# A scheduled graph-layer kernel: own PSUM tiles for the first group, held end products, rows two ahead, sums and normalising at other times, and idle turns of the identity

## The chip, the cores and the metric

The kernel runs on one core of one Trainium2 chip. The metric is the device time of one execution in microseconds (us). Several executions of each kernel were timed. "Same" is a difference of less than 2%.

## The reference

A graph layer on x of shape (32, 512, 256) with a 0/1 matrix adj of (32, 512, 512), all in float32:

```python
h = jnp.maximum(_layernorm(x, axis=-1), 0.0)
xc = jnp.transpose(h, (0, 2, 1))
c = relu(_bn(_conv1d(xc, conv1_w, 0), ...))          # 256 -> 256, 1 tap
c = _bn(_conv1d(c, conv2_w, 8), ...)                 # 256 -> 256, 17 taps
x_conv = jnp.transpose(relu(c + xc), (0, 2, 1))
s = h @ w_se.T + b_se                                # 3 columns
dist = sq[:, :, None] + sq[:, None, :] - 2.0 * einsum('bnd,bmd->bnm', s, s)
A = jnp.exp(-dist) * adj
msg = relu(h @ w_msg.T + b_msg)
x_nmp = einsum('bnm,bmd->bnd', A, msg)
x_in = concatenate([x_conv, x_nmp], -1)
gi, gh = x_in @ w_ih.T + b_ih, h @ w_hh.T + b_hh     # 3 gates of 256 each
r, z = sigmoid(gi_r + gh_r), sigmoid(gi_z + gh_z)
n = tanh(gi_n + r * gh_n)
return x + (1 - z) * n + z * h
```

## The kernel before

The 17-tap convolution is done in seven groups of 25 products with transformed inputs and weights. Around the products stand four other kinds of work for TensorE: **begins** (a batch is normalised and turned into hT), **rows** (conv1 for the batches of a group), **graphs** (messages, exponentials, and the sum over neighbours, xnb) and **gates**. A small scheduler, run while the program is built, decides the order in which all of this is written down: it keeps a clock `now` of TensorE's planned time, and each stream tells it either a time or a condition before which it must not go on. On the chip every engine then works through its own list in that fixed order. A plan that is wrong about a time therefore becomes a wait.

The first group's products share one tile of two PSUM banks. Later groups make a middle product (copied to `mid` by ScalarE) and then two "end" products:

```python
if g == 0:
    two = cps.tile([P, 2, N], F32, name="ps_c")
...
    if g == 0:
        ps, mid = two[:, n % 2, :nz], None
        product(ps[:, :nh], (0, *d0), (1, *d1))
        hand()                      # sums of the product before
        yield now
        product(ps[:, nh:], (0, *d1), (1, *d2))
    else:
        psb = bps.tile([P, N], F32, name="ps_b")[:, :nh]
        product(psb, (2, x2[:, 1, :], 0))
        mid = cv.tile([P, NH], F32, name="mid", bufs=2)[:, :nh]
        act.activation(mid, psb, AF.Copy)
        hand()
        yield now
        ps = cps.tile([P, 2, N], F32, name="ps_c")[:, :, :nh]
        for k in range(2):
            product(ps[:, k, :], (k, XD[m][:, k, :], 0))
```

hT goes through DRAM: GpSimd issues the store when a batch is begun, SyncE issues the load when the rows of its group are due. When a batch is normalised is decided by `norm_ahead`:

```python
def begin(b):
    ...                                          # b >= TURNED
    for o in range(ND):
        dve.transpose(HT[b][:, o, :], xb[:, o, :])
    nc.gpsimd.dma_start(HD[b], HT[b])            # store hd<-hT
    begun = b + 1

def all_rows():
    ...
    for g in range(1, NG):
        for b in batches(g):
            yield lambda: freed >= g - 1 and begun > b
            rows_wait = True
            load_row(b)                          # load hT<-hd on SyncE's queue
            yield now + 8.0
            yield from rows(g, b)
            rows_wait = False

def norm_ahead(early=0.45):
    for b in list(NORMS)[:2]:
        if (b < G or clock["conv"] >= (b - G) / PER - early) and norm_some(b):
            return True
    return False

streams = {
    "rows": (all_rows(), 1e9, -2.0),
    "begins": (all_begins(), 1.05 * PER, -0.15),
    "graphs": (all_graphs(), 11.5 * PER, 0.0),
    "conv": (convolution(), 80.0, 0.0),
    "gates": (all_gates(), 31.25 * PER, 1.6),
}
```

The stream that may go on and has the smallest clock goes next; the last number is where its clock starts.

## Time and profile before

| | before |
|---|---|
| time, 3 runs when the prediction was made | 2156.06 us median, 2148.67 to 2158.63 |
| span of the profiled run | 2155.2 us |
| matmul work, every record at its undisturbed spacing | 2007 us |
| loss (span less that work) | 148 us |

How to read it: TensorE is the bound, and the prediction below shows its lines of the profile. The busy share (96%) is too kind, because a matmul at half clock counts as busy for twice as long. The number used in this document is therefore the **loss**: the length of a stage less the matmul work done in it, each matmul record at the spacing that it has in the trace when nothing disturbs it. The stages are those of the prediction: to the first product, the groups, and the end.

### The profile page before, as it was taken

How to read it: one execution, taken by the hardware profiler on the slowest of the kernel's cores; microseconds unless marked ns; L12 is line 12 of the kernel's file. 1: busy time of each engine (PE TensorE's matmuls, PEld its weight loads, DVE VectorE, ACT ScalarE, POOL GpSimd, SP SyncE). 2: the span in 40 equal slices, each digit the busy share in tenths (PEclk: the TensorE clock that was granted, in tenths of full speed). 3: DMA queues.
4: the chain of work that ended last, by engine and by line, in shares of the span. 5: the costliest groups of instructions: out<-in, count | busy, mean ns of one | idle time of the engine just before them, and what ended most of it. 6: DMA issues, size and time to landing. Idle time of an engine off the chain costs nothing. (4 is left out here: it accounts for less than half of the span.)

```text
span 2155.2 us, 25648 instructions
## 1 busy us (share of the span) xinstructions
PE 2062.0 (96%) x8632; PEld 1259.6 (58%) x8632; DVE 1512.9 (70%) x2660; ACT 762.4 (35%) x1271; POOL 336.7 (16%) x582
## 2 busy tenths in 40 slices
PE   8888799999998999999999999999999999999998
PEld 4776465665654566665656655665656666654443
DVE  6777478777876667886777776877767777754333
ACT  5534533235322425233344234442242522143111
POOL 2100112112111112110121111111110211111111
PEclk9999899999999999999999999999999999999999
DMA  7335776676767658777577677676745656544331
GB/s 276 142 132 173 256 225 183 197 214 189 245 167 191 185 154 227 208 211 208 145 214 201 178 215 208 184 208 172 214 118 156 192 147 167 161 123 99 93 93 40
DMA packets 546436, 383.07 MB, mean 178 GB/s; under 512 B 456576, under 2 KB 473472, under 8 KB 545664
## 3 DMA queue, kind: packets, MB, share of 16 engines
q1 hardware_dynamic: 512992, 282.17, 49.5%
q0 software_dynamic: 28624, 86.01, 11.5%
q10 hardware_dynamic: 4688, 13.24, 1.6%
q8 instruction: 69, 1.13, 0.2%
q14 instruction: 63, 0.52, 0.1%
HBM read 281.95 MB, written 99.35 MB: 177 GB/s over the span
## 5 line engine op out<-in xcount | busy, mean ns | idle before, releaser
L135 PE MATMUL ps_acc<-xnb,wih 128*128 128x512 f32 (+1 forms) x772 | 364.9, 595 | 6.9 <-DMA xnb<-nd 6.9
L135 PE MATMUL ps_acc<-xconv,wih 128*128 128x512 f32 (+1 forms) x772 | 363.4, 593 | 2.7 <-ACT xconv L126 2.7
L135 PE MATMUL ps_acc<-hTb,whh 128*128 128x512 f32 x768 | 355.9, 593 | 1.0 <-ACT r L126 1.0
L135 PE MATMUL ps_c<-xd,w 128*128 128x135 f32 (+1 forms) x2400 | 308.3, 282 | 19.2 <-DVE n L126 9.0
L135 PEld LDWEIGHTS ps_c<-xd,w 128*128 128x128 f32 x2400 | 294.0, 193 | 22.3 <-issue 14.3
L1012 POOL DMA_DIRECT2D out_dram<-res x252 | 163.8, 657 | 771.8 <-DVE res L126 651.2
L135 PEld LDWEIGHTS ps_acc<-xnb,wih 128*128 128x128 f32 x772 | 143.1, 191 | 163.8 <-issue 149.3
L135 PEld LDWEIGHTS ps_acc<-xconv,wih 128*128 128x128 f32 x772 | 143.7, 190 | 160.7 <-issue 154.9
L135 PEld LDWEIGHTS ps_acc<-hTb,whh 128*128 128x128 f32 x768 | 141.8, 190 | 156.0 <-issue 146.4
L135 PE MATMUL ps_g<-at,msg 128*128 128x512 f32 x512 | 226.6, 592 | 1.8 <-DVE at L126 1.8
L135 PEld LDWEIGHTS ps_b<-x,w 128*128 128x128 f32 x1200 | 160.3, 191 | 67.2 <-issue 54.2
L126 DVE TENSOR_TENSOR r<-ps_acc,r 128x512 f32<-128x512 f32 (+1 forms) x65 | 44.4, 683 | 212.1 <-PE ps_acc L135 212.1
L135 PE MATMUL ps_b<-x,w 128*128 128x135 f32 (+1 forms) x1200 | 164.9, 280 | 7.7 <-ACT at L126 3.6
L135 PEld LDWEIGHTS ps_g<-at,msg 128*128 128x128 f32 x512 | 96.2, 190 | 117.5 <-issue 112.4
L126 ACT ACTIVATE mid<-ps_b 128x270 f32<-128x270 f32 (+1 forms) x150 | 59.7, 398 | 261.9 <-PE ps_b L135 261.7
L126 DVE SCALAR_TENSOR_TENSOR x<-x,x 128x544 f32<-128x544 f32 (+5 forms) x161 | 137.6, 855 | 2.9
L126 DVE TENSOR_TENSOR msg<-ps_g,bmsg 128x256 f32<-128x256 f32 x128 | 53.8, 421 | 113.1 <-PE ps_g L135 112.4
L135 PE MATMUL ps_g<-hT,w 128*128 128x512 f32 (+4 forms) x288 | 124.1, 576 | 4.8 <-DMA hT<-hd 3.7
L126 DVE TENSOR_TENSOR x<-x 128x272 f32<-128x272 f32 (+5 forms) x280 | 127.7, 497 | 0.3
L126 ACT ACTIVATE z<-ps_acc,brz 128x512 f32<-128x512 f32 x64 | 43.9, 687 | 233.3 <-PE ps_acc L135 225.2
L135 PE MATMUL ps_g<-wmsg,hTg 128*128 128x259 f32 x496 | 125.9, 382 | 0.0
L135 PE MATMUL ps_c<-x,w 128*128 128x116 f32 x800 | 105.5, 289 | 20.9 <-ACT z L126 9.9
(112 smaller groups left out, 2582.4 us busy)
## 6 DMA issues: line engine op xcount, KB each, us to landing
w<-wd SPq DMA_DIRECT2D x125, 768.0 KB, 5.7
m_sb<-in_adj_dram SPq DMA_DIRECT2D x384, 64.0 KB, 3.1
hd<-hT POOLq DMA_DIRECT2D x32, 512.0 KB, 5.6
hT<-hd SPq DMA_DIRECT2D x32, 512.0 KB, 5.5
hTb<-hd SPq DMA_DIRECT2D x32, 512.0 KB, 5.1
xnb<-nd SPq DMA_DIRECT2D x64, 256.0 KB, 3.3
xconv<-cd SPq DMA_DIRECT2D x32, 512.0 KB, 5.3
res<-in_x_dram SPq DMA_DIRECT2D x256, 64.0 KB, 3.1
```

Of the source, the lines that this page charges most:

```text
L126: getattr(self.engine, name)(*tiles, **more)
L135: nc.tensor.matmul(ps, lhsT, rhs, **more)
L1012: queue.dma_start(OB[b][:, s.start // 32 : s.stop // 32, o * P + 32 * g : o * P + 32 * g + 32], y[at, s].rearrange("i (k j) -> i k j", j=32),)
```

## The change

Its intent is to close the holes on TensorE in the first third. Its short description names five things: the first group's products in their own tiles, the end products held until their banks are free, rows loaded two ahead, graph sums ahead, and the identity turned while TensorE waits. The diff has more than that: a new rule for when a batch is normalised (`told` is the number of batches whose messages are made), a limit on how many parts stand before their stores, and two moves in the gates.

```diff
-    cps = ctx.enter_context(tc.tile_pool(name="cps", bufs=1, space=PSUM))
+    first_ctx = ExitStack()
+    cps = first_ctx.enter_context(tc.tile_pool(name="cps", bufs=2, space=PSUM))
...
+    def keep_warm(n):
+        for _ in range(n):
+            nc.tensor.transpose(unused[:, :P], ident, ident)
...
     def load_row(b):
-        HR[b] = front.tile([P, ND, N], F32, name="hT", bufs=2)
-        nc.sync.dma_start(HR[b], HD[b])
+        if b not in HR:
+            HR[b] = front.tile([P, ND, N], F32, name="hT", bufs=2)
+            nc.sync.dma_start(HR[b], HD[b])
+            HR_AT[b] = now + 8.0
...
-        if now < t or act.free > now + 0.3:
+        if now < t or act.free > now + 0.3 or len(PARTS) > 2 and now < PARTS[-3]:
             return False
...
+        act.free += 0.7
+        PARTS.append(act.free + 4.0)
...
                 sums.send(got)
+                handed = dve.free + LAG
...
-            if g == 0:
-                two = cps.tile([P, 2, N], F32, name="ps_c")
+            if g == 1:
+                first_ctx.close()
+                cps = ctx.enter_context(tc.tile_pool(name="cps2", bufs=1, space=PSUM))
...
-                    ps, mid = two[:, n % 2, :nz], None
+                    ps, mid = cps.tile([P, N], F32, name="ps_c")[:, :nz], None
...
                     hand()
-                    yield now
+                    yield handed
                     ps = cps.tile([P, 2, N], F32, name="ps_c")[:, :, :nh]
...
-    def norm_ahead(early=0.45):
+    def norm_ahead():
         for b in list(NORMS)[:2]:
-            if (b < G or clock["conv"] >= (b - G) / PER - early) and norm_some(b):
+            if (b < G or told >= b - 3) and norm_some(b):
...
                 rows_wait = True
-                load_row(b)
-                yield now + 8.0
+                for k in (b, b + 1):
+                    if k in batches(g) and k < begun:
+                        load_row(k)
+                yield HR_AT[b]
                 yield from rows(g, b)
-                rows_wait = False
+                del HR[b]
+                rows_wait = b + 1 in HR
...
-        "graphs": (all_graphs(), 11.5 * PER, 0.0),
+        "graphs": (all_graphs(), 11.5 * PER, -0.5),
...
+    keep_warm(16)
...
+            waits += 1
+            if waits > 2 and not HB:
+                keep_warm(2)
```

Left out: a flag `turning` that keeps a row from starting in the middle of a begin; in the first batch's gates a pause of 8 us and the hidden products set ahead of the residual; the same new rule where `norm_ahead(0.25)` was called; and a new planned length of a matmul (`max(0.223, 0.005 + elements / 600)` in place of `max(0.22, elements / 600)`), which shifts every planned time a little.

More of the change, by code (lines that the diff above doesn't have):

```diff
@@ L133, in matmul @@
         nonlocal now
-        now += max(0.22, elements(ps) / 600.0)
+        now += max(0.223, 0.005 + elements(ps) / 600.0)
         nc.tensor.matmul(ps, lhsT, rhs, **more)
@@ L158, in settle @@
             LATER.pop(0)[1]()
-    XS, HT, HB, HR, HG, XN, XR = {}, {}, {}, {}, {}, {}, {}
+    XS, HT, HB, HR, HR_AT, HG, XN, XR = {}, {}, {}, {}, {}, {}, {}, {}
     NORMS, NORM_AT = {}, {}
@@ L639, in summed @@
         yield
-    EVAC = []
+    EVAC, PARTS = [], []
     def batches(g):
@@ L665, in evacuate @@
         if o == ND - 1 and last == U:
-            evacuated[b] = act.free + 4.0
+            evacuated[b] = PARTS[-1]
         return True
@@ L705, in convolution @@
     def convolution():
-        nonlocal at_product
+        nonlocal at_product, cps
         def product(ps, *terms):
@@ L720, in product @@
                 )
-        done = None
+        done, handed = None, 0.0
         def hand():
-            nonlocal done
+            nonlocal done, handed
             if done is not None:
@@ L880, in begin @@
     def begin(b):
-        nonlocal begun
+        nonlocal begun, turning
         if b >= TURNED:
@@ L894, in begin @@
             HT[b] = front.tile([P, ND, N], F32, name="hT", bufs=2)
+            turning = True
             for o in range(ND):
@@ L899, in begin @@
             nc.gpsimd.dma_start(HD[b], HT[b])
-            begun = b + 1
+            begun, turning = b + 1, False
             if b + 2 < B:
@@ L907, in begin @@
         yield NORM_AT[b]
+        turning = True
         for d in range(ND):
@@ L910, in begin @@
             if d == ND - 1:
-                begun = b + 1
+                begun, turning = b + 1, False
                 if b < 2 or b >= G:
@@ L962, in gates @@
         load_sums(b, 1)
+        if b == 0:
+            yield now + 8.0
         hT = HB[b]
@@ L1049, in gates @@
             ps_r = acc.tile([P, N], F32, name="ps_acc")
+            ps_h = None
             if o == 0:
-                if b not in XC:
-                    yield lambda: b in evacuated
-                    yield evacuated[b]
-                    load_conv(b)
-                yield XC_AT[b]
-                residual(b)
-                yield from products(ps_r, o, 0, 0, 1, (0, 2))
+                if b not in RES:
+                    yield from products(ps_r, o, 0, 0, 1, (0, 2))
+                    ps_h = acc.tile([P, N], F32, name="ps_acc")
+                    yield from products(ps_h, o, 2, 0, 1, (0, 0))
+                    if b not in XC:
+                        yield lambda: b in evacuated
+                        yield evacuated[b]
+                        load_conv(b)
+                    yield XC_AT[b]
+                    residual(b)
+                else:
+                    yield from products(ps_r, o, 0, 0, 1, (0, 2))
                 yield lambda: RES[b] < 1e9
@@ L1063, in gates @@
             yield from products(ps_r, o, 0, 1, 3, (0, 2), reset)
-            ps_h = acc.tile([P, N], F32, name="ps_acc")
-            yield from products(ps_h, o, 2, 0, 1, (0, 0), reset_hidden)
+            if ps_h is None:
+                ps_h = acc.tile([P, N], F32, name="ps_acc")
+                yield from products(ps_h, o, 2, 0, 1, (0, 0), reset_hidden)
+            else:
+                reset_hidden()
             ps_z = acc.tile([P, N], F32, name="ps_acc")
@@ L1108, in background @@
         nonlocal turn_of
-        if norm_ahead(0.25):
+        if norm_ahead():
             return True
@@ L1139, in all_begins @@
             yield from begin(b)
-    rows_wait = False
+    rows_wait = turning = False
     def all_rows():
@@ L1150, in all_rows @@
             for b in batches(g):
-                yield lambda: freed >= g - 1 and begun > b
+                yield lambda: freed >= g - 1 and begun > b and not turning
                 if b == batches(g)[0]:
@@ L1154, in all_rows @@
                 rows_wait = True
-                load_row(b)
-                yield now + 8.0
+                for k in (b, b + 1):
+                    if k in batches(g) and k < begun:
+                        load_row(k)
+                yield HR_AT[b]
                 yield from rows(g, b)
-                rows_wait = False
+                del HR[b]
+                rows_wait = b + 1 in HR
     def all_gates():
@@ L1177 @@
     hold = {name: None for name in streams}
+    unused, waits = acc.tile([P, N], F32, name="ps_acc"), 0
+    keep_warm(16)
     load(0)
@@ L1214 @@
         name = min(able, key=lambda k: clock[k])
+        waits = 0
         hold[name], began = None, now
```

## The prediction

> **What bounds the kernel now.** I read the page first (shares, slices), then a table of busy time by stage, then TensorE's waits by stage, then the order of time around single waits.
>
> The page's shares and two rows of its 40 slices (one slice is 54 us):
>
> ```profile
> PE 2062.0 (96%) x8632; PEld 1259.6 (58%) x8632; DVE 1512.9 (70%) x2660; ACT 762.4 (35%) x1271; POOL 336.7 (16%) x582
> ...
> PE   8888799999998999999999999999999999999998
> ...
> PEclk9999899999999999999999999999999999999999
> ```
>
> TensorE is the bound, but not evenly: all slices that are not full lie in the first third. I cut the span at the products' groups (the last of the first group's 25 products ends at 223.6 us, of the second's at 484.7, of the third's at 781.6; from 1899.2 only graph sums and gates are left). Columns: stretch, length, busy time of TensorE, its weight loads, VectorE, ScalarE, GpSimd (instructions), granted clock, DMA share, GB/s.
>
> ```profile
> 0.00:46.50 46.50, 36.69 (x117) 19.53 (x118) 28.80 (x83) 30.48 (x63) 10.47 (x31) 0.96 0.77 282
> 46.50:223.60 177.10, 152.31 (x1020) 128.18 (x1019) 134.45 (x271) 78.03 (x148) 16.36 (x28) 0.95 0.47 159
> 223.60:272.00 48.40, 37.25 (x111) 19.05 (x111) 25.11 (x44) 25.49 (x40) 6.75 (x12) 0.86 0.72 240
> 272.00:484.70 212.70, 200.39 (x996) 136.46 (x995) 167.83 (x310) 66.49 (x119) 40.84 (x72) 0.99 0.71 207
> 484.70:781.60 296.90, 274.93 (x1130) 167.17 (x1129) 213.92 (x368) 103.44 (x178) 46.37 (x76) 0.97 0.68 190
> 781.60:1899.20 1117.60, 1112.73 (x4649) 675.55 (x4649) 836.33 (x1419) 395.24 (x639) 170.91 (x291) 1.00 0.67 185
> 1899.20:2155.20 256.00, 247.69 (x620) 113.70 (x618) 106.45 (x169) 63.25 (x85) 45.00 (x72) 0.99 0.37 91
> ```
>
> Length less busy time gives TensorE's idle time by stage: 9.8, 24.8, 11.2, 12.3, 22.0, 4.9, 8.3; in all 93. The first 781.6 us hold 80 of it; the last 8.3 are the drain after the last matmul. Busy time hides more, because it also counts time in a reduced clock. So I weighed every matmul by its undisturbed distance to the next one in this trace (429 ns for a record of 512 columns, 219 for 259, 115 for 135, 112 for 116, 109 for a transpose; a matmul is two records, a transpose one). That sums to 2007 us. The span is 148 us longer: 19 before the first product, 40 in the first group, 34 in the second (with the passage from 223.6 to 272), 32 in the third, 15 in all the rest, 8 in the drain. **What a change can win lies in the first 782 us, about 125 us.**
>
> Who ends the waits there (line, who was waited for: us, times, longest):
>
> ```profile
> PE ps_c L135 <- ACT z L126: 9.9, 13, 2.5
> PE ps_c L135 <- DVE n L126: 9.0, 3, 4.4
> PE ps_c L135 <- ACT n L126: 7.7, 10, 2.5
> PE ps_g L140 <- ACT x_sb L126: 7.1, 1, 7.1
> PE ps_acc L135 <- DMA xnb<-nd: 6.9, 3, 6.3
> PE ps_b L830 <- ACT right L126: 6.3, 2, 5.0
> PE ps_c L135 <- issue: 5.1, 2, 2.7
> PE ps_g L135 <- DMA hT<-hd: 3.7, 1, 3.7
> ...
> PE ps_c L135 <- DVE z L126: 3.4, 1, 3.4
> ```
>
> The first and third line all fall in the first group. One such wait in the order of time:
>
> ```profile
> 77.95 1.94 PE L135 MATMUL ps_c<-x,w 128*128 128x116 f32 x16
> ...
> 79.92 0.56 ACT L126 ACTIVATE z<-ps_c 128x464 f32<-128x464 f32 x1 [3.75 <-PE ps_c L135]
> ...
> 80.53 2.04 PE L135 MATMUL ps_c<-x,w 128*128 128x116 f32 x16 [0.65 <-ACT z L126]
> ```
>
> The copy of the product before starts only when the first half (16 records) of this product is done, and the second half waits for that copy: 0.56 us plus about 0.1. Both products share one tile of two banks; the recorded dependencies are the tile's, not the bank's.
>
> **What the Trainium skill says.** (1) "PSUM — Partial Sum Buffer", section on bank collisions: two engines must be kept apart by bank and quadrant; different banks run clean. So the 0.65 us wait is not one the chip needs, and two tiles of one bank each remove it. The trace cannot show the rule itself; it shows the wait. (2) "TensorE: Matmul & The Clock Gate", Part 1: after an idle window of about 3.4 us the clock is halved until a busy window has passed. This trace agrees: it granted 0.50 from 147.2 to 157.4 us, after a stretch (144.0 to 147.2) with only 0.93 us of TensorE busy time, and 16 records of 116 columns then took 3.76 us in place of 1.94. (3) Same page, Part 4: transposes do not count as busy for that clock. If so, turning the identity while waiting warms nothing. This trace does not decide it, as no window in it is filled by transposes alone.
>
> **The change part by part.**
> Own tiles: 23 waits, 9.9 + 7.7 = 17.6 us, become none, because a tile is written again only two products later. I count 15 won, as a faster TensorE meets VectorE more often.
> Ends held (the two end products are issued only when the sums have taken the last pair out of its bank): the same waits in the second and third group, "DVE n" 9.0, "issue" 5.1, "DVE z" 3.4, and 1.7 for ps_b, together 19. The hold only lets gates or sums go first; VectorE's backlog behind it (4.4 us at 596 to 600) stays. I count 12.
> Passage 223.6 to 272: the 5.0 us wait for "right" came about because ScalarE, which works in order, stood before it at a part whose buffer was still being stored (waits of 0.16 and 1.35 us for that transfer, 1.3 us for each part). The change issues a part only when its buffer should be free. Then 2.7 for the first residual (now after the hidden products) and 1.2. In the new order the second group's first product follows the first group's last at once, with 4 transposes between, where before 12 matmuls for rows, 12 for sums, 8 for messages and 6 of the gates stood there. I count 9 of 11.2.
> Rows two ahead, graph sums ahead: the waits for hT (3.7) and for xnb (6.3 + 0.4) are transfers started too late; 10.4 us, I count 9.
> Clock: the granted share says what was lost, (1 - 0.95) x 177 = 8.9, 0.14 x 48.4 = 6.8, 0.01 x 213 + 0.03 x 297 = 11, and 1.9 at the start: 28.6. The drops follow waits of 2 us and more, most of them in the list above, so they go with these; I count 15 without any help from the identity, since other idle windows remain.
> Sum of gains: 15 + 12 + 9 + 9 + 15 = 60.
> Costs: 124 identity transposes, 38 before the first hT product and 34 more before the first group; 30 of them stand ahead of the first real transpose. The identity is ready at 1.8 us; at 109 ns each they end by 5.1, at half clock by 8.3 us, against 7.06 for the data: 0 to 1.3 us late. The other 52 stand where the plan sees TensorE idle; 2 us in all for those that sit wrongly. VectorE: I counted, by order of both programs and the measured median durations, what stands before the last product of the first group: TensorE's work there rises from 137 to 169 us, VectorE's from 147 to 158 (sums of durations, some 8% above busy time, as they overlap). In the second group they fall from 227 to 206 and from 213 to 207. So VectorE is nearly as loaded as TensorE in both, and I take off 6 us for new waits on it.
> Net 60 - 8 = 52: **2156 - 52 = 2104 us**. Check by stage: first product at 46 (31 us of work), first group 169 + 17 = 186, second 206 + 22 = 228, third 275 + 16 = 291, the remaining 1325 + 13 of loss, drain 8: 2097. The two agree within what I can claim.
>
> **Rivals.**
> R1, VectorE takes over: with the shared tile gone, products come as fast as their operands and weights do, and waits turn from "ACT n, z" to "DVE x", "ACT w", "DVE n". For: 158 against 169 us in the first group. Against: before, only 3.2 us of waits there were for operands or weights, and VectorE runs at 75% between 781 and 1899 us without stopping TensorE. Then the groups one and two win little: about 2130.
> R2, the idle time only moves: work pulled forward into the first group leaves less to fill the second, whose holds then find nothing to issue. Time about 2125.
> R3, the identity does hold the clock: most of the 28.6 us come back and the start warms earlier; about 2090.
> R4, transfers pulled ahead collide in the first 60 us (DMA share 0.77): a few us lost; 2110.
>
> **Range and chances.** The line for 2% is 2113. The floor is 2007 + 7 for the first data + 8 drain = 2022; losses of 60 to 110 us are plausible after: 2080 to 2132. Most of my weight is on the plain case, a third on R1 or R2. A slowdown would need the late, full stages to suffer, and their order hardly changes. Faster 0.64, same 0.35, slower 0.01.
>
> **What would show it.** Right: no wait of ps_c on ACT n or z near 0.65 us, those two lines under 4 us together; xnb and hT waits gone from 650 to 760; the last first-group product ends near 232 and the third group's near 750; granted clock above 0.98 up to 780. Wrong: a sum of waits on DVE over 25 us in the first 480 us (R1, R2); first real transpose after 8 us; half clock in stretches full of identity turns would confirm the skill's Part 4, full clock there would refute it. If the stages after 782 us differ by over 6 us from 1374 less the work moved ahead (about 23), I misread where the change acts.

## The result, and the profile after

All ratios in this document are the mean time of one kernel's fast runs over that of the other's in the same rounds on the same chip, so not quite the ratio of the medians quoted beside them.

| | before | after |
|---|---|---|
| time, median of 4 runs each | 2152.51 us | 2127.54 us (2125.61 to 2130.82) |
| ratio, 95% interval | | 0.9883 [0.9852, 0.9914] |
| span of the profiled run | 2155.2 | 2124.6 |
| loss | 148 | 118 |

The change makes the kernel 1.2% faster: half of the 2.4% predicted, inside the range, and "same" by the 2% line, while "faster" had the highest chance.

The page of the changed kernel, the lines that answer to those of before:

```profile
PE 2064.3 (97%) x8756; PEld 1266.6 (60%) x8756; DVE 1511.3 (71%) x2660; ACT 756.9 (36%) x1267; POOL 339.9 (16%) x582
...
PE   9999899999999999999999999999999999999998
...
PEclk9999999999999999999999999999999999999999
```

The row of slices looks mended: of the six slices below 9 in the first third, two are left. It shows nothing of what happened later, because a loss of 3% in a slice is not visible in tenths. The table by stage does (same columns as in the prediction; the stages end where the same products end):

```profile
0.00:50.70 50.70, 46.40 (x197) 30.00 (x198) 32.16 (x93) 30.92 (x64) 11.02 (x32) 0.97 0.79 285
50.70:230.80 180.10, 179.14 (x1198) 146.62 (x1197) 141.03 (x291) 91.02 (x176) 16.41 (x31) 0.99 0.54 183
230.80:272.00 41.20, 30.28 (x153) 20.63 (x152) 32.84 (x62) 14.33 (x23) 10.46 (x15) 0.88 0.74 245
272.00:462.10 190.10, 184.31 (x879) 122.17 (x878) 155.76 (x275) 71.56 (x129) 35.86 (x65) 0.98 0.75 211
462.10:754.20 292.10, 281.77 (x1167) 171.02 (x1165) 214.51 (x376) 101.31 (x169) 43.45 (x75) 0.98 0.72 197
754.20:1888.70 1134.50, 1115.56 (x4636) 674.47 (x4635) 844.11 (x1442) 398.31 (x645) 179.89 (x297) 0.99 0.67 183
1888.70:2124.60 235.90, 226.80 (x538) 101.67 (x536) 90.92 (x125) 49.40 (x63) 42.80 (x68) 0.99 0.34 86
```

In the first group TensorE now idles for 1 us (180.10 less 179.14) instead of 24.8. But in the stage from the fourth group to the seventh, which was full before (idle 4.9 us, clock 1.00), it idles for 19 us and the granted clock is 0.99. Who ends the waits:

```profile
PE ps_g L136 <- DMA hT<-hd: 23.2, 11, 4.3
PE ps_b L842 <- ACT mid L127: 6.6, 1, 6.6
...
PE ps_acc L136 <- DMA hTb<-hd: 2.8, 1, 2.8
...
PE ps_acc L136 <- DMA xnb<-nd: 2.5, 3, 1.2
...
PE ps_c L136 <- DVE z L127: 1.0, 2, 0.5
```

The waits of ps_c on ScalarE and VectorE are gone but for 1.0 us, as predicted. A new one stands on top: the load of a row's hT, 23.2 us in 11 waits where before it was 3.7 us in one. Of these, 9.9 us in 7 waits lie after 754 us; before, no wait for hT lay after 782.

The loss by stage, us, against the prediction's check by stage (first stage: 46 less 31 of work; end: the drain). The turns of the identity count as loss, since they do no work:

| stage | before | predicted | after |
|---|---|---|---|
| to the first product | 19.0 | 15 | 19.8 |
| first group | 39.8 | 17 | 10.9 |
| second group, with the passage | 33.6 | 22 | 25.6 |
| third group | 32.3 | 16 | 17.1 |
| fourth to seventh group | 14.4 | 13, with the last sums and gates | 34.9 |
| last sums and gates | 0.7 | | 0.2 |
| drain | 8.3 | 8 | 9.1 |

So the gain of the first three groups came (52 us less loss than before), and **20.5 us of it were given back between the fourth and the seventh group**, where I had predicted no change. Up to 754 us the losses sum to 73.4 us against 70 predicted; after it, to the last matmul, to 35.1 against 13.

One of the late waits in the order of time (GpSimd, SyncE's queue and TensorE; brackets give the idle time before and who ended it):

```profile
986.52 0.54 POOL L912 DMA_DIRECT2D hd<-hT  x1 [2.02 <-DVE hT L127]
...
992.31 0.34 SPq L193 DMA_DIRECT2D hT<-hd  x1
...
996.04 1.22 PE L136 MATMUL ps_g<-hT,w 128*128 128x512 f32 x1 [2.43 <-DMA hT<-hd]
```

The store of this batch's hT is issued at 986.52; the load of the same data can only be issued when the store has landed, at 992.31, 5.8 us later, and its data is there after another 3.7 us. The plan had 8 us for the load alone. TensorE stands for 2.43 us, and the clock is halved from 996.0 to 999.4; the 3.4 us before that held 1.01 us of busy time of TensorE, so they were not wholly idle. The load stands in SyncE's queue while it waits, and everything behind it stands too. The queue's own waits for this store, in the kernel before, the changed kernel, and (ahead of its place) the experiment a1:

```profile
SPq L186 <- DMA hd<-hT: 16.6, 4, 5.6
```

```profile
SPq L193 <- DMA hd<-hT: 77.7, 13, 11.9
```

```profile
SPq L193 <- DMA hd<-hT: 10.4, 2, 5.3
```

The built order says why: before, the store of batch 17 stood at product 68 and its load at product 72; in the changed kernel both stand at product 73. At the end of each group the last one to three batches are begun so late that the load follows the store at once. Of the 32 loads of rows, 11 are issued less than 8 us after the store of the same batch in the changed kernel; before, none is (a1: 1, a2: 9, b4: 13).

Not all of the 23.2 us are waits for such a load: six of the eleven waits are (13.8 us). In the other five (9.4 us) the store had landed long before, and the load itself came late in SyncE's queue. Two of these loads (663.2 and 1256.0 us) stood behind a load of x that waited 12.3 and 8.5 us for VectorE to turn a batch that was begun late; for the other three the cause was not followed up.

The passage from 230.8 to 272 did not come out as predicted either. ScalarE, in the changed kernel:

```profile
267.19 1.35 ACT L127 ACTIVATE part<-y,bn_shift,bn_scale 128x522 f32<-128x522 f32 x1 [7.24 <-DMA cd<-part]
```

A part still waits 7.24 us for a buffer that is being stored, and the copy to `mid` and TensorE behind it wait too (6.6 us, second line of the waits above). GpSimd issued a store of hT at 259.59 after 3.6 us of waiting for VectorE, and the parts' stores stood behind it in GpSimd's order until 260.1; the store that this part waits for was issued then and landed at 267.1. In all, TensorE's idle time in the passage is 10.9 us (41.20 less 30.28), where before it was 11.2.

### The profile page after: what moved, and what is told of

It reads as the page before. It is cut to its first block, busy times and chain, and to the rows that moved or that the text cites.

```text
span 2124.6 us, 25898 instructions
## 1 busy us (share of the span) xinstructions
PE 2064.3 (97%) x8756; PEld 1266.6 (60%) x8756; DVE 1511.3 (71%) x2660; ACT 756.9 (36%) x1267; POOL 339.9 (16%) x582
## 3 DMA queue, kind: packets, MB, share of 16 engines
q0 software_dynamic: 28624, 86.01, 11.8%
## 5 line engine op out<-in xcount | busy, mean ns | idle before, releaser
L136 PE MATMUL ps_c<-xd,w 128*128 128x135 f32 (+1 forms) x2400 | 303.8, 279 | 1.0 <-DVE z L127 1.0
L136 PE MATMUL ps_g<-hT,w 128*128 128x512 f32 (+4 forms) x288 | 123.6, 579 | 23.2 <-DMA hT<-hd 23.2
L127 ACT ACTIVATE h<-ps_g,bn_shift,bn_scale 128x252 f32<-128x252 f32 (+4 forms) x208 | 85.4, 486 | 102.5 <-PE ps_g L136 101.9
```

The lines of the kernel that those rows point to most:

```text
L127: getattr(self.engine, name)(*tiles, **more)
L136: nc.tensor.matmul(ps, lhsT, rhs, **more)
```

## The experiments

Twelve kernels ran, each with a correct result, in three calls of four. Each call has its own 7 runs of the kernel before on the same chip (medians 2150.97, 2152.59, 2153.09 us); each variant has 4 runs. Names that start with a, b and c belong to the three calls; between calls I compare through the kernel before.

| run | starts from | edit | median us | ratio to before [95%] |
|---|---|---|---|---|
| a1 | after | old rule for normalising | 2101.72 | 0.9765 [0.9745, 0.9784] |
| a2 | after | rows loaded one by one | 2116.06 | 0.9836 [0.9820, 0.9853] |
| a3 | after | no identity turns | 2118.86 | 0.9857 [0.9834, 0.9879] |
| a4 | before | own tiles alone | 2134.78 | 0.9919 [0.9904, 0.9934] |
| b1 | a1 | no identity turns | 2099.08 | 0.9744 [0.9725, 0.9763] |
| b2 | a1 | rows loaded one by one | 2104.50 | 0.9775 [0.9753, 0.9797] |
| b3 | after | ends not held | 2164.53 | 1.0055 [1.0031, 1.0080] |
| b4 | before | new rule for normalising | 2316.55 | 1.0761 [1.0729, 1.0793] |
| c1 | before | ends held | 2125.34 | 0.9871 [0.9856, 0.9886] |
| c2 | before | identity turns | 2155.98 | 1.0007 [0.9990, 1.0023] |
| c3 | b1 | sums not ahead | 2127.05 | 0.9872 [0.9853, 0.9891] |
| c4 | b1 | parts later | 2105.55 | 0.9779 [0.9765, 0.9794] |

### a1: the old rule for normalising

My theory after the result: the late stores come from the new rule for normalising. The rival: they come from loading rows two ahead.

```diff
-    def norm_ahead():
+    def norm_ahead(early=0.45):
         for b in list(NORMS)[:2]:
-            if (b < G or told >= b - 3) and norm_some(b):
+            if (b < G or clock["conv"] >= (b - G) / PER - early) and norm_some(b):
...
-        if norm_ahead():
+        if norm_ahead(0.25):
```

> The changed kernel with only the old rule for when a batch may be normalised (by the products' progress, not by graphs told), which in the built order puts most stores of turned rows well ahead of their loads; rows are still loaded two ahead. Theory T1 (the new rule makes stores late, so a load waits 5 to 6 us in its queue for the store and TensorE waits for hT): waits of TensorE on DMA hT fall from 23.2 us to under 8, the time falls by 8 to 20 us from the changed kernel's, to about 2112. Rival T2 (loading two ahead takes both buffers and blocks the queue): hT waits stay over 15 us and the time within 5 us of the changed kernel's 2127.

Measured: 2101.72 us, 26 us under the changed kernel and more than the 8 to 20 expected; the intervals of the ratios are far apart. No wait of TensorE for a row's hT is left, and SyncE's queue waits 10.4 us for the stores instead of 77.7 (shown above). The loss from the fourth to the seventh group falls from 34.9 to 24.2 us and that of the second and third from 42.7 to 24.3, against 5.6 more in the first. TensorE's longest wait is now another:

```profile
PE ps_acc L136 <- DMA xnb<-nd: 7.8, 3, 5.1
```

The new rule costs the change about half of what its other parts win. a1 does not return everything: of the 20.5 us given back from the fourth group on it takes back 10.7. Its fourth group alone loses 17.5 us (before 4.6, changed kernel 11.3), after waits of 5.1 us for xnb and 4.4 us for "ACT h". It is not shown that the 26 us come from the late stores alone: the rule also moves VectorE's work, and b4 below shows waits for VectorE under it.

### a2: rows loaded one by one

```diff
-                for k in (b, b + 1):
-                    if k in batches(g) and k < begun:
-                        load_row(k)
+                load_row(b)
...
-                rows_wait = b + 1 in HR
+                rows_wait = False
```

> The changed kernel with rows loaded one at a time as before, the new normalising rule kept. T1: the stores of each group's last batches still stand right before their loads, so hT waits stay over 10 us and the time within 8 us of 2127. T2: hT waits fall under 6 us and the time falls by over 10 us.

Measured: 2116.06 us, some 11 us under the changed kernel; the intervals of the two ratios just touch. The waits for hT fall to 13.2 us (5 times), the queue's waits for the stores to 43.7. So loading two ahead adds to the harm, as the rival said, but it is the smaller share: under the old rule (b2 below) it does none.

### a3: no identity turns

```diff
-        for _ in range(n):
+        for _ in range(0):
```

> The changed kernel without any identity transposes (order otherwise nearly the same). If transposes of the identity do count for the clock, as the changed kernel's record suggests (full clock from 6.1 us, with nothing but identity transposes run from 1.8 to 7.4), the first full clock comes at 13 to 14 us as before the change, half-clock windows come back within the first 230 us, and the time rises by 4 to 12 us, to 2131 to 2139. If they do not count, the first full clock stays near 6 us by chance of the window and the time falls by 0 to 3 us.

Measured: 2118.86 us (2117.58 to 2127.80), some 9 us under the changed kernel by the medians and 6 by the ratios, with overlapping intervals. Neither expectation was right: the clock did what the first said, the time what neither said. TensorE's beginning, in the changed kernel and then in a3:

```profile
1.83 5.56 PE L146 MATMUL ps_acc<-ident 128*128 128x128 f32 x30 [1.83 <-POOL mhalf L251]
...
10.01 3.60 PE L136 MATMUL ps_g<-hT,w 128*128 128x512 f32 x8
```

```profile
6.99 2.81 PE L141 MATMUL ps_g<-ident,x_sb 128*128 128x128 f32 x8 [6.99 <-ACT x_sb L127]
9.63 5.85 PE L136 MATMUL ps_g<-hT,w 128*128 128x512 f32 x8
```

Thirty turns of the identity run before the first data, and the same eight matmul records then take 3.60 us instead of 5.85. The full clock is first granted at 6.1 us instead of about 14. A window of the changed kernel (columns as in the stage table) shows the speed-up within the turns, when nothing else had yet run on TensorE: 20 turns in 4.2 us, then 12 in 1.2 us.

```profile
1.80:6.00 4.20, 4.17 (x20) 4.17 (x21) 2.18 (x9) 1.28 (x1) 1.79 (x14) 1.00 0.91 263
6.20:7.40 1.20, 1.20 (x12) 1.06 (x10) 0.38 (x4) 1.00 (x2) 0.70 (x1) 1.00 1.04 358
```

(The clock column reads 1.00 here although the turns run at half speed: the trace has no record of the clock before its first change.) So the turns do raise the clock, and still the first product does not come sooner: it starts at 50.7 us with them and at 49.9 without. The order of all other instructions is the same in both, and most of the difference (5.5 of the 6.8 us between the two profiled runs) lies after 1340 us, in waits for hT (19.7 us in a3, 23.2 in the changed kernel) and in the half-clock windows after them. Whether that is more than luck in when these windows fall is not settled here; b1 and c2 say more.

### a4: own tiles alone

```diff
-            if g == 0:
-                two = cps.tile([P, 2, N], F32, name="ps_c")
+            if g == 1:
+                first_ctx.close()
+                cps = ctx.enter_context(tc.tile_pool(name="cps2", bufs=1, space=PSUM))
...
-                    ps, mid = two[:, n % 2, :nz], None
+                    ps, mid = cps.tile([P, N], F32, name="ps_c")[:, :nz], None
```

> The kernel before with only the first group's products in tiles of their own; the instruction order after the first group is the same as before. If the sum of its waits is what they cost: waits of ps_c on ACT n and z (17.6 us) under 3, the first group's last product ends near 205 in place of 223.6, the time is 15 to 20 us under the kernel before, near 2135. If VectorE or ScalarE takes over (rival R1): half of that or less, 2144 or more, with new waits on DVE x or ACT w.

Measured: 2134.78 us, 16 us under the kernel before on the same chip. The waits of ps_c on "ACT n" and "ACT z" are gone; the first group ends at 204.2 us instead of 223.6. The prediction's 15 us for this part are confirmed, and its waits turned into no new ones on VectorE or ScalarE of that size: the first group's loss falls from 39.8 to 20.3 us.

### b1: the old rule, and no identity turns

```diff
 a1, and
-        for _ in range(n):
+        for _ in range(0):
```

> The changed kernel with the old normalising rule and without identity transposes. If what a3 showed (the identity gains nothing: first product at 49.9 us without against 50.7 with it) holds, it is 0 to 9 us faster than a1's 2101.7, about 2097. If the identity has a use that a3's other waits hid, it is slower than a1 by 3 us or more.

Measured: 2099.08 us, 2.6 us under a1 by the medians and 4.5 by the ratios, within the intervals. The first product comes at 48.9 us instead of 52.7, the losses of the other stages differ by at most 2 us. This is the fastest kernel: 2.6% faster than before and 1.4% faster than the change as it came (0.9744 over 0.9883).

### b2: the old rule, and rows one by one

```diff
 a1, and the edit of a2
```

> The changed kernel with the old rule and rows loaded one at a time. If two ahead was harmful by itself (a2 won 11 us by going back to one): as fast as a1 or faster, 2095 to 2102. If two ahead is worth something once stores are early: 2105 to 2115. No wait on DMA hT above 2 us in total in either case.

Measured: 2104.50 us, 3 us over a1, within the intervals. With early stores, loading two rows ahead is worth at most a few us. The two runs a2 and b2 together suggest that two ahead is harmful only where the second row's store is not yet done.

### b3: ends not held

```diff
-                    yield handed
+                    yield now
```

> The changed kernel with the end products issued at once, not held for the sums. If the hold does what the prediction counted (12 us of 19): waits of ps_c on DVE n, z and unnamed ones return, 8 to 19 us in the second and third group, and the time rises by 5 to 15 us, to 2133 to 2142. If the hold only reorders: within 3 us of 2127.

Measured: 2164.53 us, 37 us over the changed kernel and 0.55% slower than the kernel before ("same" by the 2% line); I had expected 5 to 15. TensorE's first waits:

```profile
PE ps_c L136 <- DVE z L127: 18.8, 7, 6.5
...
PE ps_c L136 <- DVE n L127: 8.1, 6, 2.7
```

Of these 26.9 us, 19.2 stand in groups four to seven (loss there 69.2 us, against 34.9), where the kernel before had none. So in the changed kernel the hold also covers something that the change itself brings. That late rows make the products come in a burst, so that VectorE falls behind, is my reading; no run tests it.

### b4: the new rule alone

```diff
-            if (b < G or clock["conv"] >= (b - G) / PER - early) and norm_some(b):
+            if (b < G or told >= b - 3) and norm_some(b):
```

> The kernel before with only the new normalising rule. In its built order the last two or three batches of each group from the third on are stored after the group's last product, right before their loads. T1: TensorE's waits on DMA hT rise from 3.7 us to over 15, the stages after the third group lose 10 to 30 us, time 2160 to 2185. If the late store does no harm alone: hT waits under 6 us and the time within 5 us of the kernel before's 2151.

Measured: 2316.55 us, 164 us over the kernel before, where I had expected 10 to 35. TensorE's waits:

```profile
PE ps_c L135 <- DVE z L126: 52.4, 20, 6.1
PE ps_g L135 <- DMA hT<-hd: 30.4, 12, 5.6
PE ps_c L135 <- DVE n L126: 23.6, 18, 3.3
```

The queue's waits for the stores rise from 16.6 to 87.1 us, and the loss of every stage from the fourth group on is 36 to 67 us instead of 1 to 5. The wait for hT is as predicted by the theory; that the two lines of ps_c on VectorE come to 76 us (12.4 before) is what b3 hinted at, and it is the larger part. So late stores are not all that the rule brings. This run overstates what the rule does inside the change: there the sums come earlier, so `told`, and with it the normalising, does too, and the ends are held. How the 164 us shrink to the 26 of a1 is not separated here.

### c1: ends held, alone

```diff
                 sums.send(got)
+                handed = dve.free + LAG
...
-                    yield now
+                    yield handed
```

> The kernel before with only the hold: an end product waits, in the plan, until the sums have taken the last pair. Its stores of rows stand as early as in the kernel before. As the prediction counted: of 19 us of waits of ps_c on DVE n, z, ps_b and unnamed ones in the second and third group about 12 go, time 2136 to 2144. As b3 counts in the changed kernel (37 us lost without it): 2125 or less. If the 37 us belong to the changed kernel's late rows alone: the gain here is 12 us or less and b3's excess lies in the stages after the third group.

Measured: 2125.34 us, 28 us under the kernel before on this chip: as much as the whole change. No wait of ps_c on VectorE's n or z is left. The second group from 270 us and the third:

```profile
270.00:477.00 207.00, 206.26 (x1022) 139.35 (x1020) 172.91 (x321) 72.06 (x131) 45.68 (x76) 1.00 0.74 221
477.00:745.30 268.30, 260.22 (x1106) 158.62 (x1105) 209.78 (x357) 97.69 (x166) 41.45 (x72) 0.99 0.74 204
```

Idle time falls to 0.7 and 8.1 us (12.3 and 22.0 before), and the clock from 0.99 and 0.97 of full to 1.00 and 0.99: the lower clock had followed these waits.

### c2: the identity alone

```diff
+    def keep_warm(n):
+        for _ in range(n):
+            nc.tensor.transpose(unused[:, :P], ident, ident)
...
+    keep_warm(16)
...
+            if waits > 2 and not HB:
+                keep_warm(2)
```

> The kernel before with only the identity transposes (156 of them, all before the first gates; all other instructions in the same order). Expected from a1 to b1 and from the changed kernel to a3: first full clock near 6 us in place of 14, first product 1 to 4 us later, fewer half-clock windows before 230 us, time within 6 us of 2152, rather slower at the start. If warming helps where TensorE waits much, as it does in this kernel: 5 to 12 us faster, as half-clock windows before 260 us (24 us of them before) go.

Measured: 2155.98 us, ratio 1.0007 [0.9990, 1.0023]. The full clock is first granted at 5.8 us instead of 14.0, and the first product starts at 47.1 us instead of 46.5. The half-clock time before 230 us falls from 20.5 to 10.2 us as well. An earlier full clock at the start is worth nothing here. The likely reason is that TensorE is not what sets the time before the first product: before, it is busy for 36.7 of 46.5 us there, part of it at half clock, and its matmul work there is 27.5 us.

### c3: sums not ahead

```diff
 b1, and
-        "graphs": (all_graphs(), 11.5 * PER, -0.5),
+        "graphs": (all_graphs(), 11.5 * PER, 0.0),
```

> b1 (the changed kernel with the old rule and without identity) with graph sums no longer put half a group ahead. If putting them ahead is worth what the prediction counted (the xnb waits and filling of the first group): xnb waits of 5 us and more come back, time 4 to 12 us above b1's 2099. If not: within 3 us.

Measured: 2127.05 us, 28 us over b1, where I had expected 4 to 12. Only part of it is the wait for xnb (15.6 us in 7 waits, against 7.1). At the end of the seventh group, at about the same moment (1864.6 and 1863.1 us), c3 has done 1756.5 us of its matmul work and b1 1780.5: **24 us of graph work (13.7 of it the sums) are left over for the end**. The first group shows where some of it could have stood: 150 us of work there, against 168 in b1. But the group is also 10.4 us shorter in c3, so the holes that b1 fills there are 7.5 us (loss 23.5 against 16.0). The rest of the 28 lies later: 4.4 more loss in the second group, 12.5 in the third, 10.5 less in the fourth, 11 more in the fifth to seventh, 2.6 after them. So drawing the graph work forward fills holes in several stages, and it is worth more than the waits for its own result; how much of the rest comes from the waits for xnb (8.5 us more) and hT (8.2 more) is not separated.

### c4: parts later

```diff
 b1, and
-        PARTS.append(act.free + 4.0)
+        PARTS.append(act.free + 9.0)
```

> b1 with the parts of a finished group given 9 us in place of 4 us until their buffer counts as free, as the trace showed a part in ScalarE's queue waiting 2.05 us for its buffer's store (7.24 us in the changed kernel), with mid behind it and TensorE idle for 4.6 us. If the wait is what costs: no wait of TensorE on ACT mid over 1.5 us before 300 us, time 3 to 8 us under b1's 2099. If other work only takes its place: within 3 us.

Measured: 2105.55 us, 6 us over b1, which neither expectation allowed for. The wait for `mid` in the passage falls from 4.6 to 0.5 us, but waits for "ACT h" (9.6 us instead of 6.9), "ACT xconv" (3.2) and hT (3.7) come in its place. A fixed larger margin is not the cure. The same edit on the changed kernel itself could not be run: the order that it builds deadlocks.

## Why the prediction was half right

By its own steps:

- **Own tiles, 15 us.** Right: 16 alone (a4), the two lines are gone, and the first group ended at 230.8 us (predicted near 232). With one tile per bank the 0.65 us waits went and the results stayed correct, as the prediction drew from "PSUM — Partial Sum Buffer".
- **Ends held, 12 us.** Right in mechanism and too small: 28 us alone (c1), 37 taken away from the changed kernel (b3). I had said that VectorE's backlog behind the hold stays. It did not stay: all but 1 us of the 19 us of these waits went, as gates and sums stood ready to be issued instead, and in c1 the clock that had fallen with them came back.
- **Passage, 9 of 11.2.** Wrong: 10.9 us of idle time stayed. The wait for "right" became a wait for `mid`, 6.6 us (shown above), and a load of hTb and a weight that VectorE was making came with 2.8 and 1.5 us. The part issued "when its buffer should be free" is issued by the plan's time; its store stood behind another in GpSimd's order.
- **Rows two ahead, graph sums ahead: "10.4 us, I count 9".** This is the step that failed. The wait for xnb did fall, from 6.9 to 2.5 us, but the wait for hT rose from 3.7 to 23.2. I had read the two loads of a row as the only thing that changes when hT arrives, and overlooked that the same diff changes when hT is *made*: the line in `norm_ahead`, which the change's description does not name. a1 undoes that one line and gets 26 us. That it then meets the prediction's 2104 (2101.72) is partly luck: the hold and the sums win more than was counted, and the passage, the start and the fourth to seventh group (24.2 us of loss) do worse. The sums were mis-sized the other way: moved ahead, they are worth 28 us in that kernel (c3).
- **Clock, 15 us of 28.6.** Too high: a third of it came. Up to the end of the third group the time at half clock fell from 54.6 to 34.1 us, which gives back about 10 us; from there to the last matmul it rose from 3.4 to 13.7, in windows after waits, which takes 5 again. (The start, of which the trace has no clock, is not in these figures.) The granted clock up to 780 us is 0.98, not above it.
- **Identity, 2 us of cost.** About right: 1.5 to 4.5 us (c2; b1 against a1 by the ratios), though a3 leaves up to 9 open. That it does raise the clock (rival R3) is shown by a3 and c2, and by all runs together: with the turns the full clock is first granted at 4.9 to 6.1 us (6 kernels), without them at 11.8 to 14.2 (8). That this brings time back is refuted by a3 and c2.
- **The start, 15 us of loss.** Wrong: 19.8 us, as before (19.0), and 19.0 without the turns (a3). Why was not followed up; R4 (transfers that collide in the first 60 us) is neither shown nor ruled out.
- **6 us off for VectorE.** Not needed: VectorE's waits in the changed kernel are small (the longest line for ps_c is 1.0 us). R1, VectorE as the new bound, is refuted for the change as a whole; b3 and b4 show that it would be so without the hold.
- **"If the stages after 782 us differ by over 6 us ... I misread where the change acts."** This test, set before, is the one that caught it. From the end of the third group to the end of the span it took 1370 us, against 1374 less 23 predicted: 19 us too long. Another sign failed with it: between 650 and 760 us, where no wait for hT was to be left, there are two (5.2 us).

R2 said that the idle time only moves, to about 2125, and the time agrees with it. Its reason does not: the holds of the second group found work to issue (0.5 us of waits of ps_c there). Under the old rule (a1) 18.4 us of loss go in the second and third group and 10.7 in the fourth to seventh, so much of the idle time that moved belongs to the new rule, and the rest is open.

The parts do not add: 16 (own tiles) + 28 (hold) + 28 (sums) less 26 (new rule) is 46, and the change won 25 us. They were measured in different kernels (the first two in the kernel before, the others in the changed one), and parts of the diff stand untested, the planned length of a matmul among them. The difference stays open, as do the 6 to 9 us of a3.

## What to carry to other kernels

Read the diff for every condition that decides *when* something is produced, not only for the lines that its description names: a transfer that is pulled ahead gains nothing when the data it fetches is written later. Where data goes out to DRAM and back, the plan has to hold the store and the load, here 9.5 us, and an in-order queue makes everything behind a waiting load late as well. Holding a consumer until its bank is free can be worth more than the waits that it removes, if other work stands ready: in c1 19 us of waits were counted and 28 us won, and the clock that had fallen with the waits came back. And a part that is worth something alone need not be worth the same beside the others.

## What the Trainium skill lacked or had wrong

- "TensorE: Matmul & The Clock Gate", Part 4 (cited in the prediction) has it, beside figures for bf16, that the full clock does not engage for transposes. For these fp32 turns of a 128x128 identity it did: the first 20 ran 0.21 us apart, those from 6.13 us on 0.11 us apart, with nothing but transposes on TensorE until then, and eight matmul records that follow took 3.60 us instead of 5.85.
- The same page's table "Why this matters for your kernels" advises keeping TensorE busy for 4 us or more to reach the full clock. It does not say when that is worthless: here the full clock came 8 us sooner and the ratio was 1.0007 [0.9990, 1.0023] (c2), as the start was bound by other work.
- "DMA: Bandwidth & Descriptors", section "Two DMAs through the same engine are not ordered", tells the issuer to wait for the first transfer's semaphore, which is what this program does. That section does not add that the wait also holds up what stands behind it in the issuing queue: waits for such stores made up 77.7 us of SyncE's queue here, and the store and load of 512 KB shown above took 5.8 + 3.7 = 9.5 us in a row.
